# A graph network's last layer adds its experts' rows into the output by DMA, and GATv2 leaves part of its tables to the next layer

## The chip, the cores and the metric

The kernel runs on one core of a Trainium2 chip. The core has five engines that work at the same time, each in its own order of instructions: TensorE (PE, matrix products, with its weight loads, PEld), VectorE (DVE), ScalarE (ACT), GpSimd (POOL) and SyncE (SP, which here only issues DMAs). DMAs are issued by SP, ACT or POOL and are carried out by 16 DMA engines that all of them share. The metric is the device time of one launch in microseconds; the median of the runs of the kernel before is 4463.08 us (three runs, 4459.12 to 4470.91).

## What is computed

The reference is a network of four layers on a graph of 1250 nodes (512 features each) and 21250 directed edges. Every layer has three parts: a graph convolution and a global attention, both added to the features, and then a feed-forward part (a mixture of experts) added to them. In outline:

```python
x = x + L0_gnn(norm(x), edges, edge_attr) + L0_mix(norm(x))     # three GATv2 layers; linear attention
x = x + L0_ffn(norm(x))                                         # 8 experts, by rank
x = x + L1_gnn(...) + L1_mix(...);  x = x + L1_ffn(...)
x = x + L2_gnn(...) + L2_mix(...);  x = x + L2_ffn(...)
x = x + L3_gnn(...) + L3_mix(...);  x = x + L3_ffn(norm(x))     # 32 experts, two per node
```

The change touches two of these parts, and adds a preparation to a third. One GATv2 layer takes node features `x` and does, for edges with source `src`, target `dst` and two attributes `ea`:

```python
xl, xr = x @ Wl + bl, x @ Wr + br
m      = leaky_relu(xl[src] + xr[dst] + ea @ We)
alpha  = segment_softmax(m @ att, dst)
out    = segment_sum(xl[src] * alpha, dst) + b_out
x      = relu(norm(out + x) * gamma + beta)
```

The last feed-forward part picks two of 32 experts per node by a softmax gate. Each expert takes at most C = 98 rows (1.25 times the mean, rounded up; the constant `CAP` in the kernel). A row whose expert is full is dropped:

```python
buf[dest] = x[token]                       # dest = expert * C + rank, where rank < C
o = relu(buf @ W1 + b1) @ W2 + b2          # per expert
y = segment_sum(o[dest] * weight, token)   # two rows for each node, by its gate's weights
y = where(sum of weights <= 1e-12, x, y)
```

## The kernel before

`N` is 1250, `D` 512, `NT` 10: nodes lie in ten tiles of 128 rows. `self.x` holds the features in SBUF through the whole kernel. A framework plans the order: the program's text gives each instruction a priority, the framework's planner simulates the engines and lets each of them take, at each time, the first instruction in that order that is ready in the simulation; it sets the semaphores and gives out the buffers of a pool (`bufs` is their number per tag). What each engine then has is a fixed list. An instruction that waits on the chip holds up everything behind it on the same engine, and this holds for the queues of SP, ACT and POOL too.

**GATv2** (`gatv2_fast`, `gat_layer`). There are 47 groups (`FG`) of four tiles of 128 edges, sorted by target; four groups serve one block of up to 107 target nodes (`BN`; 12 blocks, `NB`). Two tables lie in DRAM for each layer: `tl`, by source, with 513 columns (`x @ Wl` and one logit term), and `tr`, by target (`x @ Wr` as a rounded part and its rest). Step `i` of the loop handles edge tile `i`. `load(g)` gathers the source rows of a group on POOL, four indirect DMAs, three groups ahead, and at the first group of a block fetches the block's rows of `tr` on SP as `hl`. `fields(g)` fetches, on SP, two descriptions of a group: `nb` (which targets an edge does not have) and the edge attributes into `oh`. It runs two groups ahead. `onehot(g)` turns `nb` into the selecting matrix on ACT; `right` multiplies it with `hl` on PE into one of three `mm` banks of PSUM; `logits` adds and reduces on DVE (for odd `i` under 20 PE does the addition, `on_pe`). `spread` makes the softmax's arguments of a group, and at a block's last group `turn` and `mix` follow from a queue named `edge`: PE sums the block's rows. `finish` queues the normalisation in `todo`; its last step, `across`, turns the block's rows, and for each node tile that is now complete it appends the ten steps of `gat_tables` for the next layer to `late`: four products with `Wl`, `left` (evacuation and store to `tl`), four products with `Wr`, `right` (store to `tr`). They use the PSUM tag `tab`, which has one bank there (`psum(3, 2, 2)` leaves 8 - 7). After the last step a `while` loop empties the three queues. The next layer's first gathers need the whole of `tl`; its `hl` of a block needs only that block's rows of `tr`. `prepare` is a generator that issues the vectors, the next layer's weights and its linear terms, a piece at every third step from step 6 on.

**Layer 1's attention** (`global_attention`) follows layer 0's expert part (`layer0_ffn`), which ends with twenty gathers `g<-l0moe_out` on POOL (L231), each followed by `add_scaled` on DVE. Its four weights and the first `ohb` loads (operands of counting work that is interleaved with the attention) are fetched before.

**Layer 3's experts** (`layer3_ffn`, L3040 on). The normalised features `xn` and the gate are computed per tile; ranks within experts come from products with a triangular matrix; `putI` holds the two places of each node, and twenty scatters (L239, two per tile) write the rows of `xn` into `routed_in` in DRAM. The gate's weights go into `w0`, the bias term and unrouted rows are added to `x`. Then for each expert: ACT issues the load of its 98 rows `xe` (three buffers), PE turns them (L3164), PE multiplies with the first matrix (L179, `feat`), ACT applies relu, PE multiplies with the second (L3173), ACT evacuates to `o` and issues the store to `routed_out`. The weights, two of 1 MB each per expert, come on SP into eleven buffers; `load` fetches the next two as soon as theirs are free. After the last expert, twenty gathers (L231) fetch two rows per node from `routed_out`, DVE adds them with their weights (L1811), and SP stores the ten tiles of `x` to `out`. `evac` alternates between ACT and DVE; in the expert loop `xT` falls to DVE and `o` to ACT.

Of the kernel before, what the change touches and what calls it, by code (L numbers as in the profile page):

```python
# [23 lines left out]
N = 1250  # L24
D = 512
# [32 lines left out]
class Net:  # L58
# [1150 lines left out]
    def gat_layer(self, L, p, xtab, otab, big):  # L1209
# [27 lines left out]
        step = [0]  # L1237

# [16 lines left out]
        def fields(g):  # L1255
            nb = p.tile([128, GE * 128], BF16, tag="nb", name="nb", bufs=4)
            nc.sync.dma_start(nb, self.nbt[g])
            s = p.tile([128, GE * 128], F32R, tag="oh", name="oh", bufs=3)
            nc.sync.dma_start(s[BW:K].bitcast(F32),
                              self.eat[:, g * GE * 128:(g + 1) * GE * 128])  # L1260
            G.setdefault(g, {}).update(nb=nb, s=s)
# [99 lines left out]
        def finish(b):  # L1361
# [44 lines left out]
            def across():  # L1406
# [10 lines left out]
                for t in whole:  # L1417
                    for f in self.gat_tables(nxt, p, t, lambda c, t=t: X[t][:, c, :],
                                             lambda: self.bank("tab", [128, D])):
                        late.append((step[0] + 1, f))  # L1420
# [37 lines left out]
        fields(1)  # L1458
        onehot(0)
        prepared = prepare()  # L1460
        for i in range(FT + 3):
# [9 lines left out]
            if j == 2 and g + 2 < FG:  # L1471
                fields(g + 2)
            if i >= 6 and i % 3 == 0:
                next(prepared, None)
# [19 lines left out]
        bias_cur(NB - 1)  # L1494
        while edge or todo or late:
            for _ in range(2):
                if edge:
                    edge.popleft()[1]()
            for _ in range(2):
                if todo:  # L1500
                    todo.popleft()[1]()
            for _ in range(2):
                if late:
                    late.popleft()[1]()
        return nxt
# [300 lines left out]

    def add_scaled(self, t, psum, gate):

        r = rows(t)
        x = self.x[:r, t, :]  # L1810
        self.nc.vector.scalar_tensor_tensor(x, psum[:r], gate[:r], x, op0=ALU.mult, op1=ALU.add)  # L1811


    def global_attention(self, xn, xnT, steps):
# [3 lines left out]
        with self.tc.tile_pool(name="ga", bufs=3) as big, \  # L1818
# [5 lines left out]
            wk = self.weight(I["L1_mix_WkT"], 4, D)  # L1824
            kT = large([128, 4, NP])
# [1210 lines left out]
    def layer3_ffn(self):  # L3036
        nc, I = self.nc, self.I
        NE, ROWS = 32, 32 * CAP
        with self.tc.tile_pool(name="l3f", bufs=1) as p, \
# [15 lines left out]
            xn = p.tile([128, NT, D], F32, name="xn")  # L3055
# [9 lines left out]
            for t in range(NT):  # L3065
                self.norm_tile(t, xn[:, t, :])
# [19 lines left out]
            getI = p.tile([128, NT, 2], I32, name="getI")  # L3086
            G = p.tile([128, NT, NE], F32, name="G")
            with self.tc.tile_pool(name="l3r", bufs=1) as pr1:
# [35 lines left out]
                for t in range(NT):  # L3124
                    r = rows(t)
                    for j in range(2):
                        self.scatter(self.rin, putI[:r, t, j:j + 1], xn[:r, t, :], "moe")
                for j in range(2):
# [4 lines left out]
                nc.vector.tensor_scalar(dest, dest, float(ROWS - 1), None, op0=ALU.min)  # L3133
                nc.vector.tensor_copy(getI, dest)
# [7 lines left out]
                                        op=ALU.mult)  # L3142
                for j in range(2):
# [3 lines left out]
            for t in range(NT):  # L3147
# [7 lines left out]
                self.add_scaled(t, xn[:, t, :], none[:, t:t + 1])  # L3155
            for e in range(NE):
                w1, w2 = ws[2 * e], ws[2 * e + 1]
                er = slice(e * CAP, (e + 1) * CAP)
                xe = tmp.tile([CAP, D], F32, tag="xe", name="xe", bufs=3)
                nc.scalar.dma_start(xe, self.rin[er, :])  # L3160
# [14 lines left out]
                o = tmp.tile([CAP, D], F32, tag="o", name="o")  # L3175
                self.evac(o, y)
                nc.scalar.dma_start(self.rout[er, :], o)
# [4 lines left out]
            for t in range(NT):  # L3182
                for j in range(2):
                    g = tmp.tile([128, D], F32, tag="g", name="g", bufs=4)
                    self.gather(g, self.rout[:, :], getI[:, t, j:j + 1])
                    self.add_scaled(t, g, w0[:, t, j:j + 1])
                r = rows(t)
                nc.sync.dma_start(self.out[t * 128:t * 128 + r, :], self.x[:r, t, :])
# [69 lines left out]
```

## Time and profile before

One execution was profiled. Its own time was 4489.82 us, its span 4487.9 us; the runs without a profile have a median of 4463.08 us.

| | us |
|---|---|
| median of the runs before | 4463.08 |
| profiled execution, time | 4489.82 |
| profiled execution, span | 4487.9 |
| PE busy | 3922.2 (87%) |
| DVE busy | 2689.5 (60%) |
| ACT busy | 1622.8 (36%) |
| POOL busy | 1351.0 (30%) |
| GATv2, first gather of layers 1, 2, 3 | at 319.67, 758.60, 1184.78 |
| GATv2, last logits of layers 1, 2, 3 | at 706, 1131, 1563 |
| layer 0's last expert gathers | 1815.8 to 1844 |
| layer 3's scatters | 4173.1 to 4199 |
| layer 3's experts on PE | 4203.2 to 4443.4 |
| layer 3's last gathers and stores | 4443.4 to 4487.9 |

How to read it: times are microseconds from the span's start. A line of the timeline has its start, its length, engine and source line (SPq is SP's queue of issues), the operation, the tile written and the tiles read, the number of instructions, and in brackets how long the engine had been idle and what ended that. PE records an fp32 product of 128x512 as two instructions. In a table by stage each row is a stretch of time with the busy time of PE, PEld, DVE, ACT and POOL, each with its number of instructions, then the granted TensorE clock, the mean busy share of the DMA engines, and GB/s. An engine that issues a DMA isn't counted as busy with it, POOL's indirect ones apart.

### The profile page before, as it was taken

What the parts mean: (1) busy time and instruction counts of PE and PEld (TensorE: products, weight loads), DVE (VectorE), ACT (ScalarE), POOL (GpSimd) and SP (SyncE); (2) the same over time, 40 slices, a digit from 0 to 9 for tenths busy, and PEclk for the clock granted to TensorE, in tenths of its full rate; (3) what the DMA queues carried; (4) which work ended last, traced back from release to release, by engine and by line L of the source; (5) the groups of instructions that cost most, each with busy time, mean ns of one, the idle gap of its engine ahead of it and who ended that gap; (6) DMA issues with size and microseconds to landing.
All of it is one profiled execution on the core that took longest, in us unless ns stands there. A gap on an engine that the chain in (4) does not pass through costs nothing. (4 is left out here: it accounts for less than half of the span.)

```text
span 4487.9 us, 49486 instructions
## 1 busy us (share of the span) xinstructions
PE 3922.2 (87%) x15466; PEld 2415.7 (54%) x15466; DVE 2689.5 (60%) x6338; ACT 1622.8 (36%) x2976; POOL 1351.0 (30%) x1308
## 2 busy tenths in 40 slices
PE   5987998899788867799999999997979896898796
PEld 3434554455354434444788877563546562455474
DVE  5357895888398865523896767314584225687301
ACT  2222442344133375110464446223451232554121
POOL 2017773776466501102000000103131013675102
PEclk9988999999899988899999999999989998997798
DMA  6437664666466423402421110383002653666695
GB/s 220 159 84 211 198 199 150 198 197 193 141 179 189 145 74 108 119 17 64 146 70 42 46 35 29 143 298 128 12 27 83 233 189 119 182 200 199 225 339 181
DMA packets 283001, 647.58 MB, mean 144 GB/s; under 512 B 61673, under 2 KB 108905, under 8 KB 267322
## 3 DMA queue, kind: packets, MB, share of 16 engines
q1 hardware_dynamic: 169290, 357.13, 24.1%
q0 software_dynamic: 73088, 234.75, 18.3%
q10 hardware_dynamic: 40352, 52.44, 3.4%
q8 instruction: 127, 2.08, 0.2%
q14 instruction: 144, 1.18, 0.1%
HBM read 528.87 MB, written 120.65 MB: 145 GB/s over the span
## 5 line engine op out<-in xcount | busy, mean ns | idle before, releaser
L231 POOL DMA_INDIRECT xl<-xl,srcI x564 | 616.8, 1094 | 290.2 <-issue 137.8
L1353 PE MATMUL more<-xl,wT 128*128 128x512 f32 x1128 | 579.7, 601 | 14.5 <-ACT wT L1343 14.0
L1286 PE MATMUL mm<-hl,oh 121*128 121x512 f32 x564 | 419.1, 743 | 73.8 <-DVE s L1299 37.8
L1302 DVE SCALAR_TENSOR_TENSOR junk<-s,att 128x512 f32<-128x512 f32 x534 | 417.9, 783 | 6.8
L1299 DVE TENSOR_TENSOR s<-xl,mm 128x512 f32<-128x512 f32 x534 | 357.8, 679 | 104.0 <-PE mm L1287 48.4
L2129 PE MATMUL more<-hh,e 128*128 128x259 f32 x1600 | 383.7, 385 | 11.7 <-ACT o L2072 8.6
L2129 PEld LDWEIGHTS more<-hh,e 128*128 128x128 f32 x1600 | 295.1, 191 | 75.8 <-issue 17.8
L171 PE MATMUL mm<-w,xnT 128*128 128x512 f32 x640 | 307.8, 620 | 16.6 <-ACT xnT L2388 12.1
L231 POOL DMA_INDIRECT hs<-gcn_h,srcI x188 | 214.6, 1142 | 93.6 <-issue 30.8
L1353 PEld LDWEIGHTS more<-xl,wT 128*128 128x128 f32 x1128 | 196.1, 192 | 74.8 <-issue 27.9
L1287 PE MATMUL mm<-hl,oh 121*128 121x512 f32 x564 | 236.4, 419 | 0.0
L1286 PEld LDWEIGHTS mm<-hl,oh 121*128 121x128 f32 x564 | 111.0, 197 | 215.5 <-issue 117.1
L231 POOL DMA_INDIRECT g<-routed_out,getI x60 | 67.6, 1126 | 488.5 <-DMA routed_out<-o 416.4
L2049 ACT ACTIVATE e<-r,hh 128x512 f32<-128x512 f32 (+1 forms) x240 | 154.2, 646 | 130.7 <-PE more L2129 119.5
L171 PEld LDWEIGHTS mm<-w,xnT 128*128 128x128 f32 x640 | 123.4, 198 | 144.0 <-issue 124.6
L3011 PE MATMUL more<-hl,oh 128*128 128x512 f32 x376 | 161.5, 534 | 30.9 <-DVE oh L2975 10.9
L1273 ACT ACTIVATE oh<-nb 112x512 fp32r<-112x512 bf16 x141 | 88.7, 630 | 273.6 <-DMA nb<-nbt 162.3
L2052 ACT ACTIVATE e<-r,a 128x512 f32<-128x512 f32 (+1 forms) x240 | 152.3, 646 | 71.1 <-DVE e L2054 57.8
L711 PE MATMUL more<-ohs,ohb 128*128 128x512 bf16 x564 | 137.5, 383 | 42.8 <-ACT ohs L695 18.0
L2054 DVE TENSOR_TENSOR e<-e,e 128x512 f32<-128x512 f32 (+1 forms) x240 | 141.5, 596 | 51.2 <-ACT e L2049 44.8
L1287 PEld LDWEIGHTS mm<-hl,oh 121*128 121x128 f32 x564 | 112.4, 199 | 110.1 <-issue 108.4
L1166 PE MATMUL tab<-w,xT 128*128 128x512 f32 x320 | 163.5, 605 | 9.0 <-ACT xT L1415 6.1
(631 smaller groups left out, 7787.8 us busy)
## 6 DMA issues: line engine op xcount, KB each, us to landing
w<-L_ffn_Wp SPq DMA_DIRECT2D x64, 1024.0 KB
w<-L_ffn_table SPq DMA_DIRECT2D x56, 1025.0 KB
neg<-ntab SPq DMA_DIRECT2D x80, 320.0 KB
nb<-nbt SPq DMA_DIRECT2D x141, 128.0 KB
hl<-xr SPq DMA_DIRECT2D x36, 448.0 KB
xr<-tro SPq DMA_DIRECT2D x30, 512.0 KB
xe<-routed_in SPq DMA_DIRECT2D x56, 256.0 KB
routed_out<-o ACTq DMA_DIRECT2D x56, 256.0 KB
```

The lines of the kernel that those rows point to most:

```text
L171: self.nc.tensor.matmul(p, lhsT=xT[:, c, t * 128:(t + 1) * 128], rhs=w[:, c, n0:n0 + n], start=c == 0, stop=c == k - 1)
L231: self.nc.gpsimd.indirect_dma_start(out=out, out_offset=None, in_=table, in_offset=bass.IndirectOffsetOnAxis(ap=idx, axis=0), bounds_check ...
L1166: nc.tensor.matmul(d[name], lhsT=xT(c), rhs=L[name][:, c, :], start=c == 0, stop=c == 3)
L1286: nc.tensor.matmul(m, lhsT=s, rhs=hl[:K, 0, :], start=True, stop=False)
L1287: nc.tensor.matmul(m, lhsT=s, rhs=hl[:K, 1, :], start=False, stop=not on_pe(i))
L1299: nc.vector.tensor_tensor(o, d["xl"][:, j, :D], s, op=ALU.add)
L1302: nc.vector.scalar_tensor_tensor(junk, s, 0.0, L["att"], op0=ALU.max, op1=ALU.mult, accum_out=d["lg"][:, j:j + 1])
L1353: nc.tensor.matmul(B[b]["y"], lhsT=d["wT"][:, j, :], rhs=d["xl"][:, j, :D], start=k == 0 and j == 0, stop=last and j == GE - 1)
L2049: nc.scalar.activation(e1[:, :n], R[q, k, 0][:, :n], AF.Exp, bias=HH[q][:, s, 256:257])
L2052: nc.scalar.activation(e2[:, :n], R[q, k, 1][:, :n], AF.Exp, bias=heads[q][0][:, s, 0:1])
L2129: nc.tensor.matmul(ys[j], lhsT=e[:, j * 128:(j + 1) * 128], rhs=HH[q][:, s, :], start=s == 0, stop=s == NT - 1)
L3011: nc.tensor.matmul(y, lhsT=oh, rhs=hl[:, i], start=i + j == 0 and not (self.fast and k), stop=last and i + j == GE)
```

## The change

It has three parts.

In `gat_layer` the second half of the table steps (`fs[5:]`: the products with `Wr` and their store) of the last three node tiles is put into a list, `rest`, instead of the queue `late`. The next layer runs the list after its first loads and before its loop. Table products that start in the ending loop take a bank of the tag `mm` instead of `tab`. Fields are fetched three groups ahead instead of two, with five `nb` and four `oh` buffers instead of four and three. `prepare` goes on from step 15 instead of 6.

In layer 3, rows are routed with two more columns: the node's number as an integer, and a zero. They go to an array of their own, `rin3`, whose unused rows name nodes beyond the real ones, so that `out` gets 128 spare rows behind 1280. Each node has a row in a table of gates, `gtab`: its first expert and its two weights. `x` is stored to `out` before the expert loop, tile by tile, on ACT. Each expert gathers the gates of its rows by the numbers that came with them, forms their weights on DVE, multiplies its result with them on the way out of PSUM, and adds it into `out` with an indirect DMA on POOL that accumulates. The gathers, additions and stores after the loop are gone, and `routed_out` is not used there.

In layer 1, `clear_places` makes the two arrays, and fills `rin3`, the spare rows of `gtab` and of `out`: 34 DMAs on SP, after the first weight load of `global_attention`.

```diff
@@ gat_layer
         def fields(g):
-            nb = p.tile([128, GE * 128], BF16, tag="nb", name="nb", bufs=4)
+            nb = p.tile([128, GE * 128], BF16, tag="nb", name="nb", bufs=5)
...
-            s = p.tile([128, GE * 128], F32R, tag="oh", name="oh", bufs=3)
+            s = p.tile([128, GE * 128], F32R, tag="oh", name="oh", bufs=4)
...
                 for t in whole:
-                    for f in self.gat_tables(nxt, p, t, lambda c, t=t: X[t][:, c, :],
-                                             lambda: self.bank("tab", [128, D])):
+                    fs = self.gat_tables(nxt, p, t, lambda c, t=t: X[t][:, c, :],
+                                         lambda: self.mm() if ending[0] else
+                                         self.bank("tab", [128, D]))
+                    if t >= NT - 3:
+                        rest.extend(fs[5:])
+                        fs = fs[:5]
+                    for f in fs:
                         late.append((step[0] + 1, f))
...
         fields(1)
+        fields(2)
         onehot(0)
+        for f in L.pop("rest", ()):
+            f()
         prepared = prepare()
...
-            if j == 2 and g + 2 < FG:
-                fields(g + 2)
-            if i >= 6 and i % 3 == 0:
+            if j == 2 and g + 3 < FG:
+                fields(g + 3)
+            if i >= 15 and i % 3 == 0:
                 next(prepared, None)
...
         bias_cur(NB - 1)
+        ending[0] = True
...
+        if nxt is not None:
+            nxt["rest"] = rest
         return nxt
@@ new, called in global_attention after the load of L1_mix_WkT
+    def clear_places(self, p):
+        nc = self.nc
+        self.rin3 = self.dram.tile([32 * CAP, D + 2], F32, name="routed_in3")
+        self.gtab = self.dram.tile([NP + 128, 4], F32, name="gates3")
+        zero = p.tile([128, D + 2], F32, name="zero3")
+        nc.gpsimd.memset(zero, 0.0)
+        nc.sync.dma_start(self.gtab[NP:, :], zero[:, :4])
+        nc.sync.dma_start(self.out[NP:, :], zero[:, :D])
+        nc.gpsimd.iota(zero[:, D:D + 1].bitcast(I32), pattern=[[0, 1]], base=NP,
+                       channel_multiplier=1)
+        for e in range(32):
+            nc.sync.dma_start(self.rin3[e * CAP:(e + 1) * CAP, :], zero[:CAP])
@@ layer3_ffn
-            xn = p.tile([128, NT, D], F32, name="xn")
+            xn = p.tile([128, NT, D + 2], F32, name="xn")
+            nc.gpsimd.memset(xn[:, :, D:], 0.0)
+            nc.gpsimd.iota(xn[:, :, D].bitcast(I32), pattern=[[128, NT]], base=0,
+                           channel_multiplier=1)
...
-                        self.scatter(self.rin, putI[:r, t, j:j + 1], xn[:r, t, :], "moe")
+                        self.scatter(self.rin3, putI[:r, t, j:j + 1], xn[:r, t, :], "moe")
+
+                nc.vector.tensor_tensor(
+                    prod, ohs[0], self.iota[:, :NE].unsqueeze(1).to_broadcast([128, NT, NE]),
+                    op=ALU.mult)
+                nc.vector.memset(gate, 0.0)
+                nc.vector.tensor_reduce(gate[:, :, 0], prod, AX.X, ALU.add)
...
-                nc.vector.tensor_scalar(dest, dest, float(ROWS - 1), None, op0=ALU.min)
-                nc.vector.tensor_copy(getI, dest)
...
+                nc.vector.tensor_copy(gate[:, :, 1:3], w0)
+                nc.sync.dma_start(self.gtab[:NP, :].rearrange("(t p) c -> p t c", p=128), gate)
...
-                self.add_scaled(t, xn[:, t, :], none[:, t:t + 1])
+                self.add_scaled(t, xn[:, t, :D], none[:, t:t + 1])
+                r = rows(t)
+                nc.scalar.dma_start(self.out[t * 128:t * 128 + r, :], self.x[:r, t, :])
             for e in range(NE):
...
-                xe = tmp.tile([CAP, D], F32, tag="xe", name="xe", bufs=3)
-                nc.scalar.dma_start(xe, self.rin[er, :])
+                xe = tmp.tile([CAP, D + 2], F32, tag="xe", name="xe", bufs=4)
+                nc.scalar.dma_start(xe, self.rin3[er, :])
+
+                to = tmp.tile([CAP, 1], I32, tag="to", name="to", bufs=8)
+                nc.vector.tensor_copy(to, xe[:, D:D + 1].bitcast(I32))
+                g = tmp.tile([CAP, 4], F32, tag="g", name="g", bufs=8)
+                self.gather(g, self.gtab[:, :], to)
+                d = tmp.tile([CAP, 2], F32, tag="d", name="d", bufs=8)
+                nc.vector.tensor_scalar(d[:, :1], g[:, :1], float(e), None, op0=ALU.is_equal)
+                nc.vector.tensor_tensor(d[:, 1:], g[:, 1:2], g[:, 2:3], op=ALU.subtract)
+                nc.vector.scalar_tensor_tensor(d[:, 1:], d[:, :1], d[:, 1:], g[:, 2:3],
+                                               op0=ALU.mult, op1=ALU.add)
...
-                o = tmp.tile([CAP, D], F32, tag="o", name="o")
-                self.evac(o, y)
-                nc.scalar.dma_start(self.rout[er, :], o)
+                o = tmp.tile([CAP, D], F32, tag="o", name="o", bufs=3)
+                nc.vector.tensor_scalar(o, y, d[:, 1:], None, op0=ALU.mult)
+                nc.gpsimd.indirect_dma_start(
+                    out=self.out, out_offset=bass.IndirectOffsetOnAxis(ap=to, axis=0),
+                    in_=o, in_offset=None, bounds_check=NP + 127, oob_is_err=True,
+                    compute_op=ALU.add)
...
-            for t in range(NT):
-                for j in range(2):
-                    g = tmp.tile([128, D], F32, tag="g", name="g", bufs=4)
-                    self.gather(g, self.rout[:, :], getI[:, t, j:j + 1])
-                    self.add_scaled(t, g, w0[:, t, j:j + 1])
-                r = rows(t)
-                nc.sync.dma_start(self.out[t * 128:t * 128 + r, :], self.x[:r, t, :])
@@ kernel
-    out = nc.dram_tensor("out", (N, D), F32, kind="ExternalOutput").ap()
+    out = nc.dram_tensor("out", (NP + 128, D), F32, kind="ExternalOutput").ap()
```

More of the change, by code (lines that the diff above doesn't have):

```diff
@@ L1237, in gat_layer @@
         step = [0]
+        rest = []
+        ending = [False]
         def block(g):
@@ L1824, in global_attention @@
             wk = self.weight(I["L1_mix_WkT"], 4, D)
+            self.clear_places(p1)
             kT = large([128, 4, NP])
@@ L3065, in layer3_ffn @@
             for t in range(NT):
-                self.norm_tile(t, xn[:, t, :])
+                self.norm_tile(t, xn[:, t, :D])
                 xT = tmp.tile([128, 4, 128], F32, tag="xnT", name="xnT")
@@ L3085, in layer3_ffn @@
             putI = p.tile([128, NT, 2], I32, name="putI")
-            getI = p.tile([128, NT, 2], I32, name="getI")
+            gate = p.tile([128, NT, 4], F32, name="gate")
             G = p.tile([128, NT, NE], F32, name="G")
@@ L3256 @@
     r = run_bass_kernel_spmd(nc, [arrays], core_ids=[0])
-    return r.results[0]["out"]
+    return r.results[0]["out"][:N]
```

## The prediction

> **What bounds the kernel now.** I read the page's head first (which engine is busy), then the chain of work that ended last (what sets the end), then tables of busy time by stage for the stages the change touches, then the timelines of PE and of SP's queue where one GATv2 layer hands over to the next.
>
> ```profile
> span 4487.9 us, 49486 instructions
> PE 3922.2 (87%) x15466; PEld 2415.7 (54%) x15466; DVE 2689.5 (60%) x6338; ACT 1622.8 (36%) x2976; POOL 1351.0 (30%) x1308
> ```
>
> PE is busy for 87%, so time can be won only where PE stands still, or where PE work is moved into such a place. The chain's last pieces show the largest such place:
>
> ```profile
> 4439.99 3.45 PE mm L3173 x8
> ...
> 4443.46 0.59 ACT o L134
> 4444.07 2.95 DMA routed_out<-o
> ...
> 4476.85 5.24 DMA g<-routed_out,getI
> ...
> 4482.19 0.75 DVE x L1811
> ```
>
> (Start, length, piece.) PE's last product ends at 4443.4; then the last expert's store must land, and 20 gathers, 20 DVE additions and the stores of `out` follow, to 4487.9: 44.5 us with PE idle. The table by stage (busy us of PE, PEld, DVE, ACT, POOL, then granted clock, DMA share, GB/s):
>
> ```profile
> 1815.00:1850.00 35.00, 11.46 (x36) 6.20 (x36) 24.59 (x59) 2.88 (x10) 22.18 (x21) 0.58 0.80 164
> ...
> 4243.00:4407.00 164.00, 164.00 (x978) 116.14 (x977) 12.83 (x24) 43.09 (x110) 0.00 (x0) 1.00 0.96 338
> 4407.00:4443.00 36.00, 36.00 (x213) 25.32 (x211) 1.60 (x3) 9.80 (x25) 0.00 (x0) 1.00 0.14 48
> 4443.00:4488.00 45.00, 0.42 (x1) 0.00 (x0) 15.03 (x20) 0.59 (x1) 22.96 (x20) 0.56 0.58 180
> ```
>
> In the expert loop PE is full and POOL does nothing, but the DMA engines are at 0.96 until 4407; then all weights are in and they fall to 0.14. PE takes (4443.4 - 4203.2)/32 = 7.51 us per expert. Between GATv2 layers 1 and 2, PE:
>
> ```profile
> 737.65 1.88 PE L1166 MATMUL tab<-w,xT 128*128 128x512 f32 x4
> ...
> 745.97 0.57 PE L1409 MATMUL tp<-ident,h 103*128 103x103 f32 x4 [2.46 <-ACT h L1403]
> 747.23 3.70 PE L1166 MATMUL tab<-w,xT 128*128 128x512 f32 x8 [0.69 <-ACT xT L1415]
> 752.34 3.70 PE L1166 MATMUL tab<-w,xT 128*128 128x512 f32 x8 [1.41 <-DVE junk L1182]
> 765.70 0.79 PE L1286 MATMUL mm<-hl,oh 121*128 121x512 f32 x1 [9.66 <-DVE s L1299]
> ```
>
> From 709 to 741 PE works without a gap on the last blocks' mixes (L1353), with table products put between. One table's four products are eight records, 3.70 us. The evacuations `tro` at 727.1 and 742.1 tell that the tables by target of tiles 7 and 8 lie wholly in this stretch, ahead of the last block's end. Only then come the last tile's `wl` table (747.2), its store, the next layer's gathers (758.6) and its first logits (765). SP's queue at that point:
>
> ```profile
> 750.96 0.38 SPq L141 DMA_DIRECT2D w<-L_gnn_Wl  x1
> 752.31 0.33 SPq L1184 DMA_DIRECT2D xl<-tlo  x1
> ```
>
> The 1 MB of weights goes out ahead of the store that the gathers wait for: 6.3 us from the store to the first gather, against 3.8 us at the next hand-over (1180.99 to 1184.78), which has no weights to load.
>
> **What the Trainium skill says.** (1) "DMA: Bandwidth & Descriptors", Rules for kernel authors: an accumulating DMA reads its destination and writes later, so a second one on the same bytes must wait for the first's semaphore. No row of this trace accumulates; I take it that the 32 additions into `out` run one after another. (2) "Collectives: The Full Stack", The bandwidth ceiling: an add by DMA reads two sources through one ring and gets half a copy's rate. Not shown here; it prices the unknown below. (3) "DMA: Bandwidth & Descriptors", Queues, rings and completion order: each DMA engine takes turns between rings packet by packet. The trace's DMA records agree: the 196 KB store `routed_out<-o` lands 4.7 to 6.5 us after issue mostly (one 7.6) while the weights stream, 1.9 us after 4414. (4) Same page, Anatomy of one DMA: about 2 us fixed for a GpSimd DMA. Near: L239's scatters take 0.98 us on POOL and land 1.3 to 1.4 us later at a DMA share of 0.5.
>
> **The change, part by part** (against the profiled span of 4487.9, the run's own time 4489.8).
>
> *Layer 3, removed.* 44.5 us after PE's end.
>
> *Layer 3, in its place.* After the last product: `o` on DVE instead of ACT 0.65 (ACT took 0.59), POOL's issue 1.1, landing of an accumulate with the DMAs nearly idle 1.4 plus a second read, say 2.2, then what lies between the last landing and the span's end, 3.0 (the last `out` packet ended at 4484.9): 7.0 us with the waits between. Gain 37.5, if nothing in the loop lags.
>
> *Does the loop keep its 7.51 us?* One link of the chain of additions is POOL issue + landing + wake-up. POOL's issue: 1.0 (lowest) to 1.5 us (one in twenty). Landing under load, by the nearest rows: 4.7 to 6.5. The second read: 98 packets of 2 KB at 88 ns over 16 engines, 0.54 us; at the skill's half rate for the whole landing, 5. So a link is at least 5.7, at most about 11.5; I take 1.1 + 5.2 + 0.5 = 6.8. That is under 7.51, so PE stays the bound; if that cover is gone, every microsecond over 7.51 costs 32 (three `o` buffers put it off by two experts only). POOL has to do one gate gather and one addition per expert, 2 x 1.3 us, and did nothing there before; the gather needs only `xe`, loaded up to four experts ahead, so it can land well before its `o`.
>
> *DMA load of the loop.* xe stays, `routed_out` becomes an addition: +0.54 us of all engines per expert, times 28 experts to 4407 is 15 us: weights end at 4422 instead of 4407. The last is needed at 4440. Cover holds; zero. `o` moves to DVE, `xT` alternates: DVE was busy 8% there; zero.
>
> *Start of the layer.* The scatters stay POOL-bound (20 in 4173 to 4199, 1.29 us each); rows of 2056 B instead of 2048 don't matter (GATv2's gathers of 2052 B rows take the same 1.0 us). About 1.1 us of DVE for the expert number goes behind `putI`. Ten stores of `x` are issued on ACT (0.31 us each), whose queue also issues `xe`: those behind it can be late. I take +1.5 in all. Net layer 3: -36.
>
> *GATv2 hand-over.* Two tables of 3.6 us leave the stretch before the last block's end: -7.2, twice: -14.4. They and tile 9's (3 x 3.7 = 11 us) go to where PE has 1.4 + 2.5 us of gaps and 9.7 us of waiting for gathers; at cover zero, else up to 3.7 per hand-over. Ending products take `mm` banks; the `tab` bank no longer serialises: inside the same 7.2.
>
> *Weights later.* The planner issues such loads when their buffer is free, not at their step: `bl` for layer 2 left at 361, in layer 1's first tenth, and its `b_out`, `gamma` and `beta` at 695 to 745, before layer 2 began. So I count zero; if it does act, 6.3 - 3.8 = 2.5 us.
>
> *Fields ahead.* Each layer's first 24 steps last 54, 46 and 54 us, later steps 1.8 to 2.0 us each; POOL's gathers allow 24 steps in 6 x 5.35 = 32. SP waits for an `oh` buffer (a 14 us wait at 1216) with `nb` loads behind it, and ACT waits 162 us for `nb` in all. A fourth buffer helps; most of the 40 us or so over 3 layers has other causes (cold PE, DMA share 0.9 to 1.0). Bounds 0 and -25; I take -6.
>
> *Layer 1's zeros.* 32 writes of 201 KB and two small ones on SP, 34 x 0.45 = 15 us of queue. SP idles from 1818 to 1861 and the DMA engines are at 0.00 from 1850 to 1860, which hides it. One memset (0.55, as L1799) among the gathers of 1815 to 1844, where POOL sets the pace, costs; 6.4 MB beside those gathers (0.80) could add 6.4 MB at 300 GB/s = 21 us of load, some of it felt. Behind SP wait `ohb` loads from 1861 on. Bounds 0 and +12; I take +4.
>
> Sum: -36 - 14.4 - 6 + 4 = -52.4. The span becomes 4435.5. The profiled run is 26.7 us above the median of the runs; I take the same difference off the median: 4463.1 - 52.4 = 4411.
>
> **Rivals.** *A: the additions become the bound.* For: an accumulate has never been measured here and the DMA is at 0.96. Against: a slower loop unloads the DMA. With links of 8.3 us the last lands at 4215 + 32 x 8.3 = 4480.6, 4 us under 4484.9: layer 3 gives 4 instead of 36, total -20: 4443. *B: GATv2 gives nothing and the zeros collide.* For: deferred products are ahead of the next layer's first ones in order, and PE runs in order; clears lie beside the gathers. Then -36 + 0 + 9: 4436. *C: slower.* Same mechanism as A, but links of 10 us, as the half rate on the whole landing would give: 4215 + 320 + 3 = 4538, +50 in layer 3, -16 elsewhere: 4497. It decides from a link of 9.4 us on (32 x 9.4 - 270 = +31, less 16 is +15); up to 8.4 layer 3 still gains.
>
> **How the numbers follow.** Forecast 0.60, A 0.16, B 0.12, C 0.10, rest 0.02. 0.3% is 13.4 us, about what a measurement of this kernel can tell from no change. Faster: forecast, B and three quarters of A, 0.84; same: the rest of A and a little, 0.05; slower: 0.11. The forecast's own range is 4388 to 4430 (fields at -25 to zero, zeros at 0 to +12). The range, 4386 to 4452, takes in B and nearly all of A.
>
> **What would show it.** Right: no gathers after PE's last product and an end within 8 us of it; `o` multiplications every 7.5 us; PE from 3.6 us per table less before the last block's end, gathers of layers 2 and 3 some 7 us earlier after their layer's last logits; weights still issued as buffers free. Wrong: POOL waiting for the previous addition in the chain, PE waiting for an `mm` bank or `o` in the loop, DVE waiting for the gate gather, or layer 1's `g<-l0moe_out` landing later than the 4.2 us median it has now.

## The result

The change makes the kernel slower. The runs of the kernel after have a median of 4529.1 us (4523.3 to 4533.4); the runs of the kernel before, on the same chip, 4467.0. The ratio is 1.0137, with a 95% interval of 1.011 to 1.0163: +1.4%, some 62 us, where the prediction had 52 us less.

The head of the page of the kernel after, which again says how long each engine was busy:

```profile
span 4530.9 us, 49686 instructions
...
PE 3937.6 (87%) x15448; PEld 2425.3 (54%) x15466; DVE 2709.3 (60%) x6464; ACT 1610.3 (36%) x2960; POOL 1405.8 (31%) x1356
```

PE's share is what it was, 87%, so the head shows nothing. The stages do (ends of a stage's last instruction in the two profiled executions, us; a "link" below is the distance from one addition into `out` to the next):

| | before | after |
|---|---|---|
| GATv2 ends | 1587.8 | 1560.9 |
| layer 1's attention ends | 2071.0 | 2041.3 |
| layer 3's graph convolution and attention end | 4125.6 | 4093.1 |
| last scatter of layer 3 issued | 4199.0 | 4166.5 |
| PE's last product | 4443.4 | 4519.9 |
| span | 4487.9 | 4530.9 |

Up to the last scatter the kernel after is 32.5 us ahead. Not all of this is the change's: the profiled execution of the kernel before took 4489.8 us, 23 over the median of its runs, that of the kernel after 4532.7, 4 over. The tail of the kernel after, behind PE's last product, is 11.0 us instead of 44.5. In between, the expert loop (from the last scatter to PE's last product) takes 353.4 us instead of 244.4: 109 us more, 11.0 us per expert instead of 7.6.

The middle of the loop of the kernel after, in the table of busy time by stretch (busy us of PE, PEld, DVE, ACT, POOL, then granted clock, DMA share, GB/s):

```profile
4300.00:4400.00 100.00, 77.50 (x397) 52.86 (x397) 12.49 (x46) 14.27 (x40) 23.49 (x19) 0.88 0.70 224
```

Before, the same loop had PE full, a clock of 1.00 and the DMA engines at 0.96. Now PE stands still for 22 of 100 us, no engine is full, and the DMA engines have slack. So something waits. The waits of the loop (total us, times, longest):

```profile
POOL out L3227 <- DVE o L3226: 187.8, 31, 7.3
...
DVE d L3207 <- DMA g<-gates,to: 93.3, 30, 6.5
DVE to L3203 <- DMA xe<-routed_in: 87.6, 28, 7.0
PEld mm L179 <- DVE o L3226: 71.3, 13, 6.3
PE mm L179 <- DVE o L3226: 69.2, 13, 6.1
```

POOL waits for `o`, not for the previous addition. PE waits for an `mm` bank that DVE's `o` has not emptied, 13 times 5.3 us on average. And DVE, busy for 12%, waits for transfers. The timelines of DVE and PE over two experts show the order (start, length, engine and line, what; in brackets the idle time ahead and who ended it). DVE:

```profile
4206.64 0.55 DVE L136 COPY xT<-tp 128x392 f32<-128x392 f32 x1
4214.24 0.15 DVE L3203 COPY to<-xe 98x1 int32<-98x1 int32 x1 [7.05 <-DMA xe<-routed_in]
4217.48 0.15 DVE L3203 COPY to<-xe 98x1 int32<-98x1 int32 x1 [3.09 <-DMA xe<-routed_in]
4220.39 0.15 DVE L3207 TENSOR_SCALAR d<-g 98x1 f32<-98x1 f32 x1 [2.76 <-DMA g<-gates,to]
...
4221.51 0.15 DVE L3207 TENSOR_SCALAR d<-g 98x1 f32<-98x1 f32 x1 [0.64 <-DMA g<-gates,to]
...
4221.90 0.74 DVE L3226 TENSOR_SCALAR o<-mm,d 98x512 f32<-98x512 f32 x1
4229.72 0.75 DVE L3226 TENSOR_SCALAR o<-mm,d 98x512 f32<-98x512 f32 x1 [7.08 <-PE mm L3223]
```

PE in the same stretch:

```profile
4210.30 3.60 PE L3223 MATMUL mm<-w,hT 128*98 128x512 f32 x8
4213.74 2.82 PE L179 MATMUL mm<-xT,w 128*128 128x98 f32 x24
4222.70 2.03 PE L179 MATMUL mm<-xT,w 128*128 128x98 f32 x8 [6.15 <-DVE o L3226]
4224.52 5.16 PE L3223 MATMUL mm<-w,hT 128*98 128x512 f32 x8
```

One product `y` is finished at 4213.9. Its `o` comes at 4221.9, 8 us later, since work of later experts stands ahead of it in DVE's list: two `to`, which wait for `xe` loads, and two `d` (three operations each), which wait for gate gathers that in turn need these `to`. `y` keeps one of the four `mm` banks; PE fills the other three with three of the next expert's first products and stops. This repeats with every second expert: for most of the loop the additions start in turn 14 to 16 and 7 to 8 us apart.

The stalls are two thirds of the loss. The rest is in the groups of the loop (busy us and mean ns of one, behind the first bar), first after, then before:

```profile
L179 PE MATMUL mm<-xT,w 128*128 128x98 f32 x1024 | 137.6, 296 | 70.9 <-DVE o L3226 69.2 <-ACT xT L134 1.2
L3223 PE MATMUL mm<-w,hT 128*98 128x512 f32 x256 | 135.4, 679 | 0.0
```

```profile
L179 PE MATMUL mm<-xT,w 128*128 128x98 f32 x1024 | 122.2, 279 | 0.0
...
L3173 PE MATMUL mm<-w,hT 128*98 128x512 f32 x256 | 115.2, 592 | 0.0
```

The products take 15.4 + 20.2 = 35.6 us more. Right behind a stall they are slower: in PE's timeline above, eight records of L3223 took 3.60 us ahead of the stall and 5.16 behind it. The granted clock (the third number from the end) goes down there too, and comes back:

```profile
4207.00:4217.00 10.00, 9.55 (x64) 7.30 (x62) 0.35 (x2) 2.40 (x7) 2.62 (x2) 1.00 0.98 320
4222.70:4229.70 7.00, 7.00 (x19) 3.79 (x20) 0.00 (x0) 0.34 (x1) 1.55 (x1) 0.65 0.58 168
```

With 70.9 us of stalls that is 106.5 of the 109 us.

The end, in the chain of work that ended last, where the last addition starts 1.1 us after PE's last product:

```profile
4514.27 6.47 issue
...
4521.00 1.51 POOL out L3227
```

### The profile page after: what moved, and what is told of

The parts are those of the page before. It is cut to its first block, busy times and chain, and to the rows that moved or that the text cites. A ratio compares the mean times of both kernels' runs of the same rounds, so it can differ in the third digit from the quotient of the medians.

```text
span 4530.9 us, 49686 instructions
## 1 busy us (share of the span) xinstructions
PE 3937.6 (87%) x15448; PEld 2425.3 (54%) x15466; DVE 2709.3 (60%) x6464; ACT 1610.3 (36%) x2960; POOL 1405.8 (31%) x1356
## 5 line engine op out<-in xcount | busy, mean ns | idle before, releaser
L179 PE MATMUL mm<-xT,w 128*128 128x98 f32 x1024 | 137.6, 296 | 70.9 <-DVE o L3226 69.2
L179 PEld LDWEIGHTS mm<-xT,w 128*128 128x128 f32 x1024 | 131.9, 209 | 85.5 <-DVE o L3226 71.3
L2083 DVE TENSOR_TENSOR e<-e,e 128x512 f32<-128x512 f32 (+1 forms) x240 | 141.5, 596 | 50.7 <-ACT e L2078 44.4
L3000 ACT ACTIVATE hl<-hs,rec 128x512 fp32r<-128x512 f32 x188 | 130.6, 717 | 90.7 <-PE more L3040 46.8
```

Of the source, the lines that this page charges most:

```text
L179: self.nc.tensor.matmul(p, lhsT=w[:, c, f * 128:(f + 1) * 128], rhs=xT[:, c, s:s + n], start=c == 0, stop=c == k - 1)
```

## The experiments

*Theory T:* DVE's list, fixed when the kernel is built, puts `to` and `d` of later experts ahead of an earlier expert's `o`; both wait for transfers. *Rivals:* the chain of additions, one after another, sets the loop (the prediction's A and C); the supply of `xe` is too short; the loss comes from the GATv2 edits or the zeros of layer 1.

The comparisons were made in groups, each against runs of the kernel before beside them. Before itself had 4467.2 us in the first group, 4500.6 and 4497.4 in the next two and 4470.7 and 4474.7 in the last two, so ratios are compared, not times. "Loop" is from the last scatter to PE's last product, "tail" from there to the span's end, both in the profiled execution:

| run | ratio to before (95%) | loop us | tail us |
|---|---|---|---|
| before | 1 | 244.4 | 44.5 |
| after | 1.0137 (1.011 to 1.0163) | 353.4 | 11.0 |
| l3_only | 1.0164 (1.0147 to 1.0181) | 349.2 | 11.1 |
| gat_only | 0.9972 (0.9958 to 0.9986) | 245.5 | 44.4 |
| handover | 0.9984 (0.997 to 0.9997) | 244.5 | 44.3 |
| no_chain | 1.0137 (1.0116 to 1.0159) | 347.1 | 13.6 |
| o_act | 0.9946 (0.9929 to 0.9963) | 268.4 | 10.9 |
| no_gather | 0.995 (0.9932 to 0.9968) | 271.0 | 11.0 |
| xe8 | 1.0136 (1.0116 to 1.0156) | 352.6 | 11.1 |
| late_d | 0.9931 (0.991 to 0.9951) | 268.6 | 13.8 |
| row_dve | 1.015 (1.0126 to 1.0174) | 353.8 | 11.1 |
| row_act | 1.0074 (1.0053 to 1.0095) | 310.8 | 10.6 |
| row_act6 | 1.0085 (1.0067 to 1.0103) | 320.7 | 10.9 |
| row_to | 0.9965 (0.9949 to 0.9981) | 248.2 | 27.4 |
| no_chain_o_act | 0.9919 (0.989 to 0.9948) | 250.0 | 13.7 |

### Which half of the change: l3_only and gat_only

The kernel before with the diff's edits from `clear_places` on, and with its edits of `gat_layer` alone:

```diff
 l3_only:  + self.clear_places(p1) ... + compute_op=ALU.add)
 gat_only: + bufs=5 / bufs=4, fields(2), fields(g + 3), rest, ending, i >= 15
```

> The kernel before with the edits of layer 3 alone (the zeroed places in layer 1 and the longer `out` among them). Theory T (DVE's fixed order: `to` and `d` of later experts wait for transfers and stand ahead of `o`): layer 3 loses what the two traces show, so 4463 + 76 - 2 = about 4535 us (4525 to 4545). If part of the loss came from the GATv2 edits instead, it would be under 4510.

> The kernel before with the GATv2 edits alone. From the two traces GATv2 ends 26.9 us earlier: 4463 - 27 = about 4436 us (4430 to 4442). The prediction's terms were -14.4 and -6: 4443. Rival B (deferred products only move the wait) would show 4455 or more.

Layer 3's edits alone cost 1.64%, 73 us; GATv2's alone gain 0.28%, 12.5 us (6 to 19). The two add up to the whole change, so the loss is layer 3's. GATv2 gives less than both the trace of the two kernels (26.9) and the prediction (20.4) said: the expectation for it missed, and 4456 us lies just inside what it gave to rival B, though the gain is not nothing.

### Is it the chain of additions: no_chain

```diff
-                nc.gpsimd.indirect_dma_start(out=self.out, ..., compute_op=ALU.add)
+                nc.gpsimd.dma_start(self.rin[er, :], o)
```

> The changed kernel with the 32 additions into `out` replaced by 32 plain stores of `o` into separate rows of a scratch buffer, still issued by POOL; the experts' sum is left out of `out`. Rivals A and C (the chain of additions, or the second read of each): the loop comes back to 7.5 us per expert and the time to 4400 to 4430 us. Theory T: `o` is as late as before, the time stays at 4505 to 4530 us (the last landing may be a few us shorter).

No addition and no chain, and nothing is won: 1.0137, the ratio of the full change (4536.6 us, 7 over the bracket of theory T). The waits of this run's loop:

```profile
POOL routed_in L3227 <- DVE o L3226: 208.9, 32, 8.0
...
DVE d L3207 <- DMA g<-gates,to: 91.7, 30, 5.9
DVE to L3203 <- DMA xe<-routed_in: 83.4, 28, 6.1
```

They are those of the kernel after. Rivals A and C fall as the cause of the loss. In the kernel after, too, every addition but one starts 0.3 us after its `o` is done.

### Is it DVE: o_act and no_gather

```diff
 o_act:
-                nc.vector.tensor_scalar(o, y, d[:, 1:], None, op0=ALU.mult)
+                nc.scalar.activation(o, y, AF.Copy, scale=d[:, 1:])
 no_gather:
-                self.gather(g, self.gtab[:, :], to)
+                nc.vector.memset(g, 0.5)
```

> The changed kernel with one line different: ACT, not DVE, multiplies the product by its gate and writes `o`. `d` and `to` stay on DVE. Theory T: `o` and the `mm` bank no longer stand behind DVE's waits, PE's loop goes from 10.8 us per expert to 7.5 to 8.5, and the time to 4400 to 4445 us. The additions' chain (rivals A and C) isn't touched: if it sets the loop, the time stays at 4515 to 4535.

> The changed kernel without the gate gathers in the expert loop: `g` is set to 0.5 by DVE, so the gates don't reach `out`. `o`, `to` and `d` stay on DVE in a fixed order. Theory T: the waits of `d` for the gather (30, 93 us) go, those of `to` for `xe` (28, 88 us) stay ahead of `o`; part of the loss comes back: 4440 to 4500 us. If the gather alone holds DVE: 4400 to 4435. If DVE's waits don't matter: 4515 to 4535.

Either edit alone takes the loop from 353 to about 270 us and the kernel below the one before. So one of the two kinds of wait, that for the gather, carries the loss: without it `to` still waits for `xe` on DVE, and the loop is within 3 us of the one with `o` on ACT. But both runs stop at 8.4 to 8.5 us per expert, not 7.5. In the run with `o` on ACT, POOL, in the middle of the loop and at its end (DMA share 0.94 from 4250 to 4300, 0.35 from 4400 on):

```profile
4283.24 1.55 POOL L3227 DMA_INDIRECT out<-o,to  x1 [2.72 <-ACT o L3226]
4290.83 1.52 POOL L3227 DMA_INDIRECT out<-o,to  x1 [6.04 <-issue]
4298.32 1.51 POOL L3227 DMA_INDIRECT out<-o,to  x1 [5.97 <-ACT hT L3219]
...
4417.11 1.51 POOL L3227 DMA_INDIRECT out<-o,to  x1 [3.75 <-ACT o L3226]
4422.43 1.51 POOL L3227 DMA_INDIRECT out<-o,to  x1 [3.80 <-DMA out<-o,to]
```

Here an `o` waits up to 19 us for its addition, although the release is put down to other engines in most lines. From start to start the links shown are 7.6 and 7.5 us, and at the end 5.3 us. The chain that the prediction feared looks like the *next* bound, at 8.0 us per link in the mean of this run (the expectations below take 8.2).

### Depth or order: xe8 and late_d

```diff
 xe8:
-                xe = tmp.tile([CAP, D + 2], F32, tag="xe", name="xe", bufs=4)
+                xe = tmp.tile([CAP, D + 2], F32, tag="xe", name="xe", bufs=8)
 late_d (the operations of `d` moved from the top of the loop to between `y` and `o`):
-                nc.vector.tensor_scalar(d[:, :1], g[:, :1], float(e), None, op0=ALU.is_equal)
+                nc.vector.scalar_tensor_tensor(d[:, :1], y[:, :1], 0.0, g[:, :1],
+                                               op0=ALU.mult, op1=ALU.add)
+                nc.vector.tensor_scalar(d[:, :1], d[:, :1], float(e), None, op0=ALU.is_equal)
```

> The changed kernel with 8 `xe` buffers instead of 4, nothing else. If the depth of the supply is the cause (loads that go out too late for want of a buffer), loads leave four experts earlier, the row numbers and gates are there in time and the time falls to 4440 to 4470 us (ratio 0.994 to 1.001). If DVE's place for them in its list is the cause, the planner moves `to` and `d` forward with the earlier loads, so that they wait for the transfers ahead of `o` as before: ratio 1.010 to 1.017.

> The changed kernel with the gate of an expert computed after its product: the first operation of `d` reads one column of `y` (times 0.0) with the gate, so it can't be placed ahead of the product. One DVE operation of about 0.15 us more per expert; the same gathers, the same 4 `xe` buffers, `o` on DVE. In DVE's list each `d` now stands right ahead of its own `o`, two `to` still stand ahead of every second `o`. Theory T: `o` is no longer held by a later expert's gather, the loop goes to the chain's pace, and the time to that of the runs without the gather or with `o` on ACT: ratio 0.993 to 0.998. If the gather is simply too late for its own expert: 1.008 to 1.017.

Twice the `xe` buffers change nothing in the time (1.0136), but the waits of the loop are others:

```profile
DVE to L3203 <- DMA out<-o,to: 124.4, 24, 7.7
...
DVE d L3207 <- DMA g<-gates,to: 108.7, 27, 7.1
```

The planner moved `to` and `d` forward with the loads, to eight experts ahead, as the second half of the expectation says. There they meet another limit: `to` has eight buffers too, and each of the last 24 `to` starts within 0.03 us of the landing of the addition eight experts before, which frees its buffer. Its own `xe` was issued 11 to 50 us earlier. So DVE's list now ties an expert's `o` to the addition ahead of it, by way of `to`, the gather and `d`. The run shows that more `xe` buffers alone don't help; a deeper supply with more `to` buffers was not tried. What decides between depth and order is `late_d`: it keeps every transfer, every engine and every buffer, adds one small DVE operation, and binds the place of `d`: 0.9931. A stretch of its DVE:

```profile
4271.54 0.15 DVE L3203 COPY to<-xe 98x1 int32<-98x1 int32 x1 [6.46 <-DMA xe<-routed_in]
4272.24 0.15 DVE L3203 COPY to<-xe 98x1 int32<-98x1 int32 x1 [0.55 <-DMA xe<-routed_in]
4272.31 0.15 DVE L3221 SCALAR_TENSOR_TENSOR d<-mm,g 98x1 f32<-98x1 f32 x1
...
4272.94 0.75 DVE L3228 TENSOR_SCALAR o<-mm,d 98x512 f32<-98x512 f32 x1
4278.29 0.16 DVE L3221 SCALAR_TENSOR_TENSOR d<-mm,g 98x1 f32<-98x1 f32 x1 [4.60 <-PE mm L3219]
```

But for one wait of 1.7 us, no `d` waits for a gather any more; it waits for its product, and the gather has long landed. The two `to` still wait for `xe`, and `o` follows 0.7 us behind the second. Through the whole loop of this run two `to` and the expert's own `d` stand ahead of every second `o`, where the kernel after has two `to` and the `d` of two later experts. So the supply was in time all along, and the place of `d` was the cause. This is the lowest ratio of the complete kernels, 0.7% under the one before; its interval overlaps with that of `o_act`.

### Gates in the row: row_dve, row_act, row_act6, row_to

`row_dve` widens the scattered row by the expert number and both gates, and takes the index straight from `xe`; the others build on it:

```diff
 row_dve:
-                self.gather(g, self.gtab[:, :], to)
+                to = xe[:, D:D + 1].bitcast(I32)              # xe: bufs=8
+                nc.vector.tensor_scalar(d[:, :1], xe[:, D + 1:D + 2], float(e), ...)
 row_act:   + nc.scalar.activation(o, y, AF.Copy, scale=d[:, 1:])
 row_act6:  + o bufs=6, xe bufs=6
 row_to:    + nc.vector.tensor_copy(to, xe[:, D:D + 1].bitcast(I32))
            + nc.scalar.copy(xT, q)                           # o and xe: bufs=6
```

> The changed kernel with the gates and the first expert's number carried in the scattered rows (516 columns, scatters behind the gate computation), no gate table, no gate gather, no `to` (the addition takes its index from `xe`), and 8 `xe` buffers; `o` stays on DVE. DVE's only waits for transfers in the loop are `d` for `xe`, which is now loaded up to six experts ahead. Theory T: the loop falls to 7.5 to 8.0 us per expert, 4420 to 4445 us. If the chain of additions takes over at 8.2 us a link, as it seems to in the run with `o` on ACT: 4440 to 4450.

> As the one before, with `o` on ACT. POOL's loop is additions alone, three gathers of 1.4 us each no longer stand between them. Theory T with a link of 1.5 + 5.5 = 7.0 us: PE sets the loop again at 7.5 us per expert, 4418 to 4432 us. If a link stays at 8.2 us: 4440 to 4450.

> As the one before, with 6 `o` buffers instead of 3 and 6 `xe` buffers instead of 8: the additions may lag by three experts more. If links over 7.5 us while the weights stream set the loop, and shorter ones after the last weights win that back, this is 3 to 12 us faster than the one before; if PE sets the loop there, the same within 3 us.

> Gates carried in the scattered rows as in the last three runs, but the index is copied out of `xe` into `to` again (so an `xe` buffer is free once its row numbers and gates are read, and ACT's next load doesn't wait for an addition), and ACT alone writes `xT` and `o`; 6 buffers of `xe` and of `o`. No instruction that PE waits for stands behind a wait for a transfer. Theory T: the loop is PE's, 7.5 us per expert, with the additions lagging by up to six experts: 30 to 48 us faster than before (ratio 0.990 to 0.993). If the chain's links of 8.2 us still set it, 15 to 25 us faster (0.9945 to 0.9965).

The first three missed. I had taken the gather away and put the wait for `xe` in its place: an `xe` buffer is now held until the addition that reads its index has landed, so loads go out later, and `d` of experts far ahead waits for them in front of `xT` and `o`. In `row_act`, DVE and then ACT:

```profile
4359.29 0.15 DVE L3198 TENSOR_SCALAR d<-xe 98x1 f32<-98x1 f32 x1 [15.07 <-DMA xe<-routed_in]
```

```profile
4334.89 0.31 ACTq L3194 DMA_DIRECT2D xe<-routed_in  x1
4335.31 0.69 ACT L3217 ACTIVATE o<-mm,d 98x512 f32<-98x512 f32 x1 [7.04 <-DMA out<-o,xe]
```

ACT's own load waits 7 us for an addition, with `o` and `hT` behind it. More `o` buffers don't help against that (1.0085, with two `xe` buffers fewer, so the two aren't told apart). `row_to` mends both at once: the index is copied out, and nothing that PE waits for is executed on DVE. Its loop, by stretch, and its additions at the end:

```profile
4300.00:4350.00 50.00, 49.88 (x293) 34.80 (x292) 2.88 (x23) 16.34 (x40) 8.63 (x6) 1.00 0.99 336
```

```profile
4300.30 1.50 POOL L3219 DMA_INDIRECT out<-o,to  x1 [8.04 <-DVE d L3201]
...
4403.59 1.51 POOL L3219 DMA_INDIRECT out<-o,to  x1 [6.86 <-ACT o L3218]
...
4475.15 1.51 POOL L3219 DMA_INDIRECT out<-o,to  x1 [3.69 <-DMA out<-o,to]
4480.54 1.50 POOL L3219 DMA_INDIRECT out<-o,to  x1 [3.88 <-DMA out<-o,to]
```

PE is full again, at 7.8 us per expert with the start of the loop. Now the DMA engines are at 0.99, eleven links from 4300.30 to 4403.59 take 9.4 us each, and an `o` waits up to 40 us. The chain ends 27.4 us after PE. The gain of the loop is paid back at the tail, as the expectation's second half said; the ratio of 0.9965 is at its edge.

### The chain as the next bound: no_chain_o_act

Both edits, `o` on ACT and plain stores:

```diff
+                nc.scalar.activation(o, y, AF.Copy, scale=d[:, 1:])
+                nc.gpsimd.dma_start(self.rin[er, :], o)
```

> The changed kernel with `o` on ACT and the additions replaced by plain stores into separate rows; the experts' sum is left out of `out`. With `o` on ACT alone the time was 20 us under before (0.9946). If the chain of additions was what held that run: 35 to 48 us under before (0.989 to 0.992). If DVE's waits ahead of `xT` hold it: the same as with the additions, 0.993 to 0.996.

0.9919, in the chain's bracket: the loop is 250 us and PE full (49.94 of 50 us at 4250 to 4300 and at 4300 to 4350). Without the chain the tail is short too. So with DVE's order mended, the additions cost the 18 us of loop that separate 268.4 from 250.0. The edit takes away each addition's second read with the chain, so the two aren't told apart here; that the chain itself binds is seen in `row_to`, where POOL has nothing else to do and starts each addition some 9.4 us after the one before, with up to six `o` ready.

### GATv2: handover

The hunks with `rest` and `ending` alone; two groups ahead, three `oh` buffers and `i >= 6` as before.

```diff
+                    if t >= NT - 3:
+                        rest.extend(fs[5:])
+                        fs = fs[:5]
```

> The kernel before with the deferred table products of the GATv2 layers alone (fields two groups ahead and three `oh` buffers as before, weights not held back). In the traces the stretch from a layer's last logits to the next layer's first ones is 5 to 8 us shorter, twice. If that is the whole gain of the GATv2 edits (12 us, 0.9972): 0.9965 to 0.998; if fields ahead and later weights carry half of it: 0.998 to 0.9995.

0.9984, 7 us (1 to 13): at the border between the two brackets, so the split of the 12.5 us isn't settled. `gat_only` and `handover` were also measured in different groups, in which GATv2 itself ran differently (last section).

## Why the prediction was wrong

**The step that failed** is in "DMA load of the loop" and the sentence before it: "`o` moves to DVE, `xT` alternates: DVE was busy 8% there; zero", and "the gather needs only `xe` ... so it can land well before its `o`". I priced DVE by its busy share. DVE's load did stay small, 12%. But I had not asked what stands in its list ahead of `o`. The gather *can* land before its own `o`, as `late_d` shows; but the list put it ahead of another expert's. The terms were put at zero; the loop took 109 us more. With the place of `d` mended (`late_d`) it takes 24 us more than before, so the order is 85 of the 109. Of what stays, 18 us go when the additions go (`o_act` to `no_chain_o_act`): that is the prediction's "PE stays the bound", which failed too, hidden by the longer wait. The rule that the prediction's front part states, that a waiting instruction holds up everything behind it, applies to DVE too; I applied it to PE and to the queues of SP and ACT only. The prediction named "DVE waiting for the gate gather" as a sign of being wrong, but no rival had a price for it.

**The link of the chain**, 6.8 us, was too small: it is 9.4 with the DMA engines at 0.99 and 5.3 with them nearly idle. POOL's issue is 1.51, not 1.1, and an addition takes more of the engines. The shares by DMA queue in `row_to`, from 4250 to 4400, with 16 additions (q0) and 19 loads of `xe` (q10):

```profile
q0 software_dynamic: 1995, 3.13, 12.8%
q10 hardware_dynamic: 2139, 3.86, 9.1%
```

12.8% of 150 us by 16 is 1.20 us of all engines per addition. Before, the same stretch had 14.2% for 40 transfers of 196 KB, 0.53 each. The second read, with what goes with it, is 0.67, against 0.54 in the prediction. The Trainium skill ("Collectives: The Full Stack", The bandwidth ceiling) has an add read two sources and get half a copy's rate; by estimate that is 1.06 for the whole. Against the plain `xe` loads of the same stretch of `row_to`, 9.1% for 19 or 0.72 each, the addition is 1.7 times as dear, against those of before 2.3 times: the half rate lies between. In the kernel after this did not decide, since a loop of 11 us leaves room for such links. Rival C had the right sign and half of the size (+34 of +62 us) by the wrong mechanism: `no_chain` shows that its links were not the cause. The link of 9.4 us from which on, it said, it decides, is what the links come to once PE is fed; then they cost 18 us of loop or 16 us of tail, not 50.

**The tail**: forecast 7.0 in place of 44.5, measured 11.0. The saving was 33.5 instead of 37.5; the issue of 1.51 and 8.4 us from there to the span's end (5.2 forecast) make the difference.

**Start of the layer**: +1.5 forecast; from the end of layer 3's attention to the last scatter it is 73.4 us before and after.

**Zeros in layer 1**: +4 forecast, nothing found. From the end of GATv2 to the end of layer 1's attention it takes 483.2 us before, 482.9 with the zeros in `l3_only`, 485.9 without them in `gat_only`. So they cost nothing that shows, neither in SP's queue nor beside the gathers, which land 6.1 us after their issue with the zeros (`l3_only`) and 5.8 without (`gat_only`, medians).

**GATv2 hand-over**: -14.4 forecast. From a layer's last logits to the next layer's first, `l3_only` (old code) takes 63.5 and 58.3 us, `gat_only` 55.6 and 54.0: -12.2, the step as described. In the kernel after the products by target no longer lie ahead of the block's end:

```profile
734.96 0.58 PE L1411 MATMUL tp<-ident,h 103*128 103x103 f32 x4 [4.21 <-ACT h L1405]
736.23 15.48 PE L1166 MATMUL mm<-w,xT 128*128 128x512 f32 x32 [0.69 <-ACT xT L1417]
```

They follow in one block of 32 records, with the last tile's products by source. But the rest of layer 2 is 9.6 us longer in `gat_only` than in `l3_only` (330.0 against 320.4), layers 1 and 3 within 1.1; why stays open. Measured by time the hand-over is worth 7 us.

**Fields ahead**: -6 forecast, from first 24 steps of 54, 46 and 54 us. `l3_only`, with the same old code there, has 53.2, 39.8 and 39.3, and `gat_only` 51.3, 38.4 and 39.3. So most of what I meant to shorten in layers 2 and 3 belonged to the one execution I read. That execution was 27 us over the median; I took this off the total but still read its stretches as typical. The fields can have 3 us of it (53.2 - 51.3, and 39.8 - 38.4). Nor did they shorten these steps where they were long: layers 2 and 3 have 48.8 and 50.6 us in `handover`, with fields two edge groups ahead, and 55.6 and 53.4 in `row_to`, measured beside it, with three.

**Weights later**: zero forecast, and the load of `Wl` still goes out just ahead of the store that the gathers wait for (SP's queue after):

```profile
741.44 0.38 SPq L141 DMA_DIRECT2D w<-L_gnn_Wl  x1
742.79 0.33 SPq L1184 DMA_DIRECT2D xl<-tlo  x1
```

**The sum**: -33.5 for the tail, +109 for the loop, -12.5 for GATv2 by its own run, zero for the rest: +63; measured +62.

## What to carry to other kernels

When an operation moves to an idle engine, read that engine's list, not its load: ask what will stand ahead of it, what those operations wait for, and who holds a buffer meanwhile. A small operation that prepares a later iteration from a transfer belongs on an engine that nothing urgent shares, or must be bound to a place behind the urgent work; deeper buffers of one tile don't help if the planner moves the waiting operations forward with the loads, up to the next tile's last buffer. And once that wait is gone, look for the next bound: here serial additions, of 9.4 us each at full DMA load.

## What the runs showed of the hardware

An indirect addition of 98 rows of 2 KB takes POOL 1.51 us to issue, against 0.98 for a plain scatter of up to 128 such rows in the kernel before, and comes every 5.3 us at best when each waits for the one before. A gather of 98 rows of 16 bytes lands 5.7 us (median) after its issue with the DMA engines at 0.70; the small size doesn't make it quick. PE's 13 stalls in the loop, 5.3 us in the mean, cost half as much again in slower products (35.6 us beside 70.9); in the 7 us behind one of them the granted clock was 0.65, in the middle of the loop 0.88, and 1.00 before the change.

The first 24 steps of the second GATv2 layer took 38.7 us in the profiled execution of the kernel after and 55.6 in that of `row_to`, whose GATv2 code is the same. This goes with the group of the measurement, not with the code: in the profiles of the two groups in which the kernel before took 4497 to 4501 us, these steps last 49 to 56 us in the second layer and 51 to 53 in the third; in those of the other three, 37 to 40 and 38 to 39. The two layers together differ by 28 us in the mean of these profiles, which is of the size of the 23 to 33 us by which the kernel before differs between the groups. The cause is open.
